# Layer 0 of a four-layer graph network: the order of all engines made from a list of steps, and the far entries' weighting moved to ScalarE

## The chip, the cores and the metric

The kernel runs on one core of a Trainium2 chip. The metric is the device time in microseconds of one execution. In the profile's names PE is TensorE (PEld its weight loads), DVE is VectorE, ACT is ScalarE, POOL is GpSimd and SP is SyncE; SP issues most DMAs, and POOL issues the indirect ones.

## The reference, cut to what matters

`x` is 2708 x 128, `adj` is 2708 x 2708 with some 2.3% of entries other than zero. Four layers follow each other, each closed by a residual and a normalization. Only layer 0 is touched:

```python
s = node_feats @ msg_w[:, :D].T
d = node_feats @ msg_w[:, D:].T
messages = jax.nn.gelu(s[:, None, :] + d[None, :, :] + msg_b, approximate=False)
aggregated = jnp.einsum('ijd,ij->id', messages, adj)
combined = jnp.concatenate([node_feats, aggregated], axis=-1)
new_feats = combined @ upd_w.T + upd_b
h = jax.nn.gelu(new_feats, approximate=False) + node_feats
```

A gelu is taken for each pair of rows (i, j) whose `adj[i, j]` isn't zero, of `s[i] + d[j] + b`, and the results are summed over j with the weights `adj[i, j]`.

## The kernel before, in words

**Tiling.** Layer 0 works on 22 row tiles of 125 rows (5 groups of 25), and within a tile on 22 column blocks of 124 columns: 484 blocks. For each row and block the first five entries other than zero get a slot; what is past the fifth is a "far" entry, of which a row has up to sixteen, found by their values.

**One block.** PE fills one of three two-bank tiles `sl` in PSUM: `begin` (L953) writes the row's `s` into all slots, `pick` (L960) adds `d` and the weight of the chosen columns through one-hot matrices `S` (ten matmuls). ACT takes the gelu out of `sl` into `g` (L1042). DVE's `weigh` (L1026) takes the weights out of the same `sl` into `W`. `add_up` (L977), once for two blocks, sums `g` with `W` into `acc`. A slot tile is free for the next `begin` when both have read it.

**One tile ahead.** For the next row tile the columns' third `at` and the rows `ar` are loaded by SP; DVE makes `mask` (L817), PE counts ranks (L825 for columns, L866 for rows), ACT casts them to `rk` (L826), DVE makes the five slot matrices `S` of each third (L845) and the parts of the weights `dA` (L838). `past` (L877, L879) keeps the entries past the fifth in `o` and counts them, `largest_of` and `largest` (MAX8) find the sixteen largest as `v`.

**Far entries.** `where` (L915, FIND_INDEX8) finds their places, eight at a time; `start_far` (L910) loads the row's `s` eight times into one of three buffers `far`, `fetch` (L919) adds eight gathered rows of `d` by indirect DMAs from POOL, `far_gelu` (L925, ACT) follows for all eight, and `far_sum` (L931, L933) multiplies each with its weight and adds it to `extra`, one DVE instruction for each of the sixteen. `turn` (L939 to L942, PE) brings `acc` and `extra` into `aggT`, `close` (L945) copies it out. `check` (L899 to L906) counts, in eight small DVE instructions a tile, rows with more far entries than sixteen or with equal values.

**Order.** The instructions of this part stand in the order in which the program issues them. Before, a loop over the 484 blocks issues `begin` (for two blocks), `pick`, the gelu, the block before's `weigh`, then every other step whose hand-written block number has come:

```python
for n in range(OV // 8):
    yield b - 1 + n * 9, lambda n=n: self.start_far(n)
    yield b + 2 + n * 9, lambda n=n: self.fetch(n)
    yield b + 15 + n * 13, lambda n=n: self.far_gelu(n)
    for k in range(8):
        yield b + 17 + n * 13 + k // 2, lambda n=n, k=k: self.far_sum(n * 8 + k)
yield b + 36, self.turn
```

After the last block the update of all rows follows (L1007 to L1016), with the last tile's second far gelu, far sums and turn between its first steps. Layers 1 to 3 follow.

Of the kernel before, what the change touches and what calls it, by code (L numbers as in the profile page):

```python
# [14 lines left out]
F32 = mybir.dt.float32  # L15
# [7 lines left out]
P = 128  # L23
# [47 lines left out]
class Step:  # L71


    def __init__(self, engine, cost, emit, after, rank, group, ahead, table, cells, bank, then):
        self.engine, self.cost, self.emit, self.after, self.rank = engine, cost, emit, after, rank
        self.group, self.ahead, self.table, self.cells, self.bank, self.then = group, ahead, table, cells, bank, then
        self.end = None

# [94 lines left out]
def gnn_stack(ctx: ExitStack, tc: tile.TileContext, t, out: bass.AP):  # L173
# [378 lines left out]
    with ExitStack() as l0:  # L552
# [10 lines left out]
        with ExitStack() as msg:  # L563
# [28 lines left out]
            nc.vector.memset(spread, 0.0)  # L592
# [4 lines left out]
            nc.vector.tensor_copy(spread[:, :, :RG], ident[:, :LR].rearrange("p (c i) -> p c i", c=NC))  # L597

            bad = mp.tile([P, LT], F32, name="bad")
# [3 lines left out]
            with tc.tile_pool(name="pre0", bufs=1) as pp:  # L603
                trif = pp.tile([JB, P], F32, name="trif")
                nc.vector.memset(trif, 1.0)
                nc.gpsimd.affine_select(
                    out=trif[:, :JB], in_=trif[:, :JB], compare_op=ALU.is_gt, fill=0.0, base=0,
                    pattern=[[1, JB]], channel_multiplier=-1)
                nc.vector.scalar_tensor_tensor(
                    trif[:, :JB], ident[:JB, :JB], EDGE, trif[:, :JB], op0=ALU.mult, op1=ALU.add)  # L610
                nc.vector.tensor_copy(tri, trif)


# [11 lines left out]
            lp = msg.enter_context(tc.tile_pool(name="load", bufs=3))  # L625
            ap_ = msg.enter_context(tc.tile_pool(name="rowsof", bufs=3))
            mk = msg.enter_context(tc.tile_pool(name="masks", bufs=2))
            sp = msg.enter_context(tc.tile_pool(name="ranks", bufs=3))
            op_ = msg.enter_context(tc.tile_pool(name="past", bufs=1))
            gp = msg.enter_context(tc.tile_pool(name="fetch", bufs=3))  # L630
            vp = msg.enter_context(tc.tile_pool(name="values", bufs=3))
            up = msg.enter_context(tc.tile_pool(name="sums", bufs=2))
            ep = msg.enter_context(tc.tile_pool(name="slots", bufs=6))
            p_misc = msg.enter_context(tc.tile_pool(name="ps_misc", bufs=1, space=PSUM))
            p_slot = msg.enter_context(tc.tile_pool(name="ps_slot", bufs=1, space=PSUM))
            p_out = msg.enter_context(tc.tile_pool(name="ps_out", bufs=1, space=PSUM))
            sl_all = [p_slot.tile([P, 2, BANK], F32, name=f"sl{n}") for n in range(3)]
            for v in sl_all:
                nc.vector.memset(v, 0.0)
# [7 lines left out]
            xT = aggT  # L647

            def turn_x():
                for n, (a, b) in enumerate(spans(0, NT, 4)):  # L650
                    ps = sl_all[n % 3][:, n // 3, :]
                    for i in range(a, b):
                        r = rows[i]
                        nc.tensor.transpose(ps[:, (i - a) * P:(i - a) * P + r], x[:r, i, :], ident[:r, :r])
                    w = min(b * P, N) - a * P
                    (nc.scalar.copy if n % 2 else nc.vector.tensor_copy)(xT[:, a * P:a * P + w], ps[:, :w])

            class Piece:


                def __init__(self, n):
                    self.n = n
                    self.b0, self.b1 = 4 * n, min(4 * n + 4, NB)
                    self.a0, self.a1 = 4 * n, min(4 * n + 4, NT)

                def products(self):
                    b0, b1, a0, a1 = self.b0, self.b1, self.a0, self.a1
                    psd, pss = (sl_all[(2 * self.n + k) % 3][:, 0, :].rearrange("p (b d) -> p b d", d=D)
                                for k in range(2))
                    d = self.d = ep.tile([P, NC, D], F32, name="g")[:JB, :b1 - b0, :]  # L670
                    room = gp.tile([P, 8, D], F32, name="far")
                    s = self.s = room[:, :a1 - a0, :]
                    parts = room[:, 4:, :].rearrange("p i d -> p (i d)").bitcast(FP16)
                    self.parts = parts.rearrange("p (q i d) -> p q i d", q=2, d=D)[:, :, :a1 - a0, :]
                    if N < b1 * JB:
                        nc.vector.memset(d, 0.0)
                    if N < a1 * P:
                        nc.vector.memset(s, 0.0)
                    for b in range(b0, b1):
                        r = min(JB, N - b * JB)  # L680
                        nc.tensor.matmul(psd[:r, b - b0, :], xT[:, b * JB:b * JB + r], msg_d, start=True, stop=True)
                    for i in range(a0, a1):
                        nc.tensor.matmul(pss[:rows[i], i - a0, :], xT[:, i * P:i * P + rows[i]], msg_s,
                                         start=True, stop=True)
                    full = min(b1, NFB) - b0
# [4 lines left out]
                    self.hi, self.lo = (v[:, b0:b1, :, :D] for v in dA)  # L690
                    nc.scalar.activation(self.hi[:, :, 0, :], d, AF.Copy, scale=D_SCALE)
                    self.spread(self.hi)
                    for a, b, r in groups():
                        if a0 <= a < a1:
                            nc.vector.tensor_tensor(s[:r, a - a0:b - a0, :], pss[:r, a - a0:b - a0, :],
                                                    over_tiles(msg_br, b - a, r), op=ALU.add)
                    nc.scalar.activation(self.parts[:, 0], s, AF.Copy, scale=D_SCALE)
                    nc.sync.dma_start(out=s_tab[a0 * P:a1 * P, :].rearrange("(n p) d -> p n d", p=P), in_=s)
# [4 lines left out]
                def spread(self, v):  # L703

                    nc.gpsimd.tensor_copy(v[:, :, 1:, :], v[:, :, 0:1, :].to_broadcast(
                        [JB, self.b1 - self.b0, NC - 1, D]))

                def update(self):
                    ps = p_out.tile([P, PB, D], F32, name="acc")
                    u = ep.tile([P, NC, D], F32, name="g")[:, :self.a1 - self.a0, :]  # L710
                    if N < self.a1 * P:
                        nc.vector.memset(u, 0.0)
                    for a, b, r in groups():
                        if self.a0 <= a < self.a1:
                            for i in range(a, b):
                                nc.tensor.matmul(ps[:r, i - self.a0, :], xT[:, i * P:i * P + r], upd_x,
                                                 start=True, stop=True)
                            nc.vector.tensor_tensor(u[:r, a - self.a0:b - self.a0, :],
                                                    ps[:r, a - self.a0:b - self.a0, :],
                                                    over_tiles(upd_b, b - a, r), op=ALU.add)  # L720
                    nc.sync.dma_start(out=u_tab[self.a0 * P:self.a1 * P, :].rearrange("(n p) d -> p n d", p=P), in_=u)

                def rests(self):
                    b0, b1, a0, a1 = self.b0, self.b1, self.a0, self.a1
                    lo = self.lo
                    nc.vector.scalar_tensor_tensor(self.parts[:, 1], self.s, D_SCALE, self.parts[:, 0], op0=ALU.mult,
                                                   op1=ALU.subtract)
                    nc.vector.scalar_tensor_tensor(lo[:, :, 0, :], self.d, D_SCALE, self.hi[:, :, 0, :], op0=ALU.mult,
                                                   op1=ALU.subtract)
                    self.spread(lo)  # L730
                    for q in range(2):
                        nc.sync.dma_start(out=sq_tab[q, a0 * P:a1 * P, :].rearrange("(n p) d -> p n d", p=P),
                                          in_=self.parts[:, q])

            def preparation():
                yield -NB - 9, turn_x
                for n, b in enumerate((-26, -22, -14, -10, -6, -2)):
                    piece = Piece(n)
                    yield b, piece.products
                    yield b + 2, piece.update  # L740
# [1219 lines left out]
```

## Time and profile before

| | us |
|---|---|
| median of 3 runs | 1880.32 (1880.05 to 1880.57) |
| the profiled execution | 1879.03, its span 1877.3 |
| layer 0, steady part | 100 to 780 us: 414 of 484 block gelus |
| layer 0, last sums on PE | up to 857.4 us |

The page gives busy shares for the span: PE 84%, DVE 76%, ACT 53%, POOL 35%. They mix four layers with different limits, so they say little on this change; the views by stretch say more. In the strip of 40 slices each digit is the busy share of a slice in tenths; one slice is 46.9 us, and layer 0 fills the first 18 or 19. In the groups of instructions the columns are line, engine, operation, what is written from what, the count, the busy time in us and the mean of one in ns, then the idle time before them and what ended it.

### The profile page before, as it was taken

The page shows a single profiled execution, that of the slowest core. Times are in us where ns is not written, and L with a number is a line of the kernel's source. Part 1 is how long each engine was busy: PE and PEld are TensorE (multiplying, and loading weights), DVE is VectorE, ACT ScalarE, POOL GpSimd, SP SyncE. Part 2 cuts the span into 40 slices and gives each one's busy share as a digit, 9 for nine tenths or more (in the row PEclk, how much of TensorE's full clock was granted, in tenths as well). Part 3 has the DMA queues.
Part 4 walks back from the last instruction along what each step waited for, and adds up shares of the span by engine and source line. Part 5 has one row for each costly group of instructions (what it writes and reads, how often), then busy time and mean ns, then how long its engine had stood idle before and what let it go on. Part 6 is the DMA issues. An engine that isn't in the chain of part 4 may idle for free.

```text
span 1877.3 us, 36661 instructions
## 1 busy us (share of the span) xinstructions
PE 1581.1 (84%) x14033; PEld 921.2 (49%) x14033; DVE 1432.4 (76%) x3609; ACT 999.4 (53%) x1538; POOL 653.2 (35%) x429
## 2 busy tenths in 40 slices
PE   4889999999999999884799995568888897299995
PEld 4666666666666666663444442312322343044542
DVE  7899999999999999976588885748886782860104
ACT  3556666666666666544344443568886862430003
POOL 5667767777777776664100000010000100000000
PEclk9899999999999999997899998658997798599998
DMA  8757666666666766543044410032333554354431
GB/s 223 167 117 153 127 144 145 135 145 128 147 135 137 151 129 139 101 104 104 0 154 161 164 64 1 9 118 89 139 139 117 171 174 169 118 207 148 148 123 32
DMA packets 234895, 238.29 MB, mean 127 GB/s; under 512 B 28844, under 2 KB 219630, under 8 KB 228122
## 3 DMA queue, kind: packets, MB, share of 16 engines
q1 hardware_dynamic: 183670, 212.18, 36.2%
q0 software_dynamic: 51040, 23.68, 10.6%
q8 instruction: 112, 1.84, 0.4%
q14 instruction: 73, 0.60, 0.1%
HBM read 220.65 MB, written 15.15 MB: 126 GB/s over the span
## 4 chain that ended last, share of the span: by engine, by line
PE 38%; DVE 7%; ACT 6%; issue 1%; DMA 0%; ACTq 0%; DVEq 0%
PE acc L1857 11%; PE lg L1245 5%; PE acc L1252 5%; PE accV L1585 5%; PE ps L1513 4%; PE accO L1589 2%; PE ps L1568 1%; ACT arena L1519 1%; DVE arena L1547 1%; PE ps L1514 1%; ACT x L379 1%; DVE arena L1571 1%; PE ps L447 1%; PE ps_w L1213 1%; ACT arena L1540 0%
## 5 line engine op out<-in xcount | busy, mean ns | idle before, releaser
L919 POOL DMA_INDIRECT far<-d_tab,ix x352 | 583.1, 1657 | 217.3 <-issue 97.0
L1042 ACT ACTIVATE g<-sl 128x640 f32<-128x640 f32 x484 | 335.4, 703 | 297.3 <-PE sl L960 272.5
L960 PE MATMUL sl<-dA,S 124*128 124x153 f16 x4840 | 380.9, 233 | 0.0
L960 PEld LDWEIGHTS <-S 124*128 124x128 f16 x4840 | 326.0, 98 | 72.0 <-issue 69.8
L977 PE MATMUL acc<-g,W 128*32 128x128 f32 x4840 | 194.5, 280 | 15.5 <-DVE W L1026 13.5
L953 PE MATMUL sl<-s,same 50*128 50x459 f16 x968 | 150.5, 333 | 17.8 <-DVE W L1026 15.5
L977 PEld LDWEIGHTS acc<-g,W 128*32 128x32 f32 x4840 | 117.4, 109 | 70.4 <-DVE W L1026 27.5
L1026 DVE TENSOR_TENSOR W<-sl,own 128x125 f32<-128x125 f32 x484 | 131.2, 275 | 21.6 <-ACT g L1042 21.6
L1500 POOL TENSOR_TENSOR arena<-arena,off 128x128 f32<-128x128 f32 (+1 forms) x22 | 23.0, 1049 | 350.3 <-DMA arena<-in_adjT 245.1
L845 DVE TENSOR_SCALAR S<-rk 124x1000 f16<-124x1000 bf16 (+1 forms) x330 | 141.4, 455 | 0.0
L1246 ACT ACTIVATE w<-lg,row_L_gnn_gate_bias 128x512 f32<-128x512 f32 (+1 forms) x132 | 83.4, 636 | 108.2 <-PE lg L1245 107.0
L915 DVE FIND_INDEX8 ix<-v,o 128x8 uint32<-128x2728 f32 x44 | 131.8, 2994 | 0.0
L1585 PE MATMUL accV<-arena,X 128*128 128x512 f32 (+4 forms) x264 | 123.3, 587 | 6.5 <-DVE arena L1551 6.5
L1245 PE MATMUL lg<-qT,mT 128*128 128x512 f32 (+2 forms) x264 | 121.2, 548 | 3.6 <-ACT w L1246 3.1
L1252 PE MATMUL acc<-w,both 128*128 128x512 f32 (+2 forms) x264 | 121.2, 547 | 0.0
L449 DVE TENSOR_TENSOR g<-ps,row_L_gnn_b 128x512 f32<-128x512 f32 (+2 forms) x14 | 7.9, 573 | 147.4 <-PE ps L447 147.3
L933 DVE SCALAR_TENSOR_TENSOR extra<-far,v,extra 128x128 f32<-128x128 f32 x330 | 114.6, 347 | 6.8 <-ACT far L925 0.5
L1513 PE MATMUL ps<-XT 128*128 128x512 f32 (+8 forms) x150 | 91.0, 696 | 32.2 <-ACT arena L1519 26.5
L1857 PE MATMUL acc<-at,x 128*128 128x512 f32 (+2 forms) x156 | 66.2, 575 | 48.5 <-ACT x L379 48.5
L1247 DVE TENSOR_TENSOR w<-w,at 128x512 f32<-128x512 f32 (+1 forms) x132 | 82.6, 626 | 27.1 <-ACT w L1246 27.0
L877 DVE SCALAR_TENSOR_TENSOR o<-ps,ar 128x496 f32<-128x496 f32 x132 | 82.0, 621 | 12.2 <-DMA ar<-in_adj 6.8
L884 DVE MAX8 cand<-o 128x8 f32<-128x248 f32 x242 | 90.4, 412 | 0.0
(359 smaller groups left out, 2494.2 us busy)
## 6 DMA issues: line engine op xcount, KB each, us to landing
at<-in_adjT SPq DMA_DIRECT2D x42, 1354.0 KB
ar<-in_adj SPq DMA_DIRECT2D x105, 248.0 KB
far<-s_tab SPq DMA_DIRECT2D x44, 512.0 KB
at<-in_adjT SPq DMA_DIRECT2D x42, 448.0 KB
arena<-in_adjT SPq DMA_DIRECT2D x21, 704.0 KB
arena<-in_adjT SPq DMA_DIRECT2D x21, 650.0 KB
held<-in_adjT SPq DMA_DIRECT2D x7, 1354.0 KB
f_tab<-arena SPq DMA_DIRECT2D x10, 704.0 KB
```

The source lines that it names most:

```text
L845: nc.vector.tensor_scalar(self.S[h][:, :n, :, k * RG:(k + 1) * RG], self.rk[h][:, :n, :LR].rearrange("p b (c i) -> p b c i", c=NC), EDGE + ...
L915: nc.vector.max_index(ix, self.v[:, n * 8:n * 8 + 8], self.o.rearrange("p b j -> p (b j)"))
L919: nc.gpsimd.indirect_dma_start(out=self.far[n][:, k, :], out_offset=None, in_=d_tab[:, :], in_offset=bass.IndirectOffsetOnAxis(ap=self.ix[ ...
L953: nc.tensor.matmul(columns_of(sl, 0, DA)[:, a:e, :], same[p], self.s3[p, :e - a, :], start=True, stop=False)
L960: nc.tensor.matmul(columns_of(sl, 0, DA)[:, c, :], self.S[h][:, n, c, :], dA[q][:, b, c, :], start=False, stop=q == 1 and c in (2, NC - 1))
L977: nc.tensor.matmul(self.acc[q:q + 32, k, :], W[:, c, :], g[:, c, :], start=b == 0 and k == 0, stop=ends)
L1042: nc.scalar.activation(g, columns_of(sl, 0, D), AF.Gelu, scale=1.0 / D_SCALE)
L1245: nc.tensor.matmul(lg, mT[:, j * P:j * P + r], qT[:, a:b], start=True, stop=True)
L1252: nc.tensor.matmul(acc[k], mrow[:rows[j], j, :], ws[j][:rows[j], a:b], start=j == 0, stop=j == NT - 1)
L1513: nc.tensor.matmul(ps, XT[:, self.js], XT[:, c], start=True, stop=False)
L1585: nc.tensor.matmul(Pair.acc[0][:, a:b], X[:self.r, self.j, :], self.w_[:, a:b], start=first, stop=last)
L1857: nc.tensor.matmul(acc[k], src[:rows[j], j, :], at[:rows[j], a:b], start=j == order[0], stop=j == order[-1])
```

## The change

The order of layer 0's main part is no longer written by hand. Every step is added to a list with its engine, a cost, a due number and the keys that it reads and writes; `Order.run` goes through time by these costs and, whenever an engine is free, issues its ready step with the lowest due number. The costs and due numbers serve for the order alone. Buffers come from fixed lists (as many of each as before) in place of pools. The gelu and the `weigh` of a slot tile both "write" the slot's key, so `weigh` comes after the gelu in the list. `begin` is a step for each slot tile. The far entries are scaled on ACT, one instruction for each of the sixteen (`far_weigh`), and then added on DVE by halving, for both halves of a tile at once. The checks of all tiles are made once, at the last tile, from kept `v` and counts; `past` copies the raw count. Clears of `ar` and of the last third's `at` are done once on POOL at the start; `tri` is made in the room of `spread`.

```diff
+class Order:
+    LATENCY, TURN = 0.12, 0.1
+    def add(self, engine, cost, emit, due, reads=(), writes=(), lag=0.0, take=None, give=None, kind=None):
...
+    def run(self, buffers):
...
+                while mine:
+                    due, s = heapq.heappop(mine)
+                    if s.take and not (freed[s.take] and min(freed[s.take]) <= now):
+                        held.append((due, s))
+                        continue
...
+                    s.emit()
...
+            DUE = {"load": -20.5, "load_s": 25, "load_row": -11, "start_far": 153.5, "rank": -19, "rank_row": -16,
+                   "begin": -0.3, "pick": 0, "add_up": 2.5, "turn": -26.5, "out": 10, "cast": 17.5, "a_hi": 58.5,
+                   "gelu": 36, "far_weigh": 68.5, "close": 126, "far_gelu": 57, "weigh": -67, "largest": -48,
+                   "index": -38, "mask": -11, "far_sum": -34.5, "past": -5, "max": -2.5, "a_lo": 1, "S": 1,
+                   "fetch": 125}
...
-                def far_sum(self, k):
-                    w, f = self.v[:, k:k + 1], self.far[k // 8][:, k % 8, :]
-                    if k == 0:
-                        self.extra = up.tile([P, D], F32, name="extra")
-                        nc.vector.tensor_scalar(self.extra, f, w, None, op0=ALU.mult)
-                    else:
-                        nc.vector.scalar_tensor_tensor(self.extra, f, w, self.extra, op0=ALU.mult, op1=ALU.add)
+                def far_weigh(self, n, k):
+                    f = far_all[(self.t * (OV // 8) + n) % 3][:, k, :]
+                    nc.scalar.activation(f, f, AF.Copy, scale=self.v[:, n * 8 + k:n * 8 + k + 1])
+                def far_sums(self, fars):
...
+                    yield "DVE", 1.12, plus(a, a, b), keys[1], keys[0]
+                    yield "DVE", 0.61, plus(a[:, :4, :], a[:, :4, :], a[:, 4:, :]), (), keys[0]
+                    yield "DVE", 0.33, plus(a[:, :2, :], a[:, :2, :], a[:, 2:4, :]), (), keys[0]
+                    yield "DVE", 0.2, plus(self.extra, a[:, 0, :], a[:, 1, :]), keys[0], [("extra", self.t % 2)]
...
+                            add("POOL", 1.56, fetch, due + DUE["fetch"] + k,
+                                reads=[("ix", f), ("far", f), *(("d_tab", j) for j in range(6))],
+                                writes=[("far", f, k)], lag=4.5)
...
+                        add("ACT", 0.6, functools.partial(nc.scalar.activation, g_all[g], columns_of(sl_all[sl], 0, D),
+                                                          AF.Gelu, scale=1.0 / D_SCALE), block + DUE["gelu"],
+                            writes=[("sl", sl), ("g", g)])
+                        add("DVE", 0.2, functools.partial(weigh, sl_all[sl], W_all[W]), block + DUE["weigh"],
+                            writes=[("sl", sl), ("W", W)])
...
+            add("SP", 0.1, U.load, (LT - 1) * NB + 7, reads=[("u_tab", n) for n in range(6)],
+                writes=[("o", m) for m in range(-(-NB // PB))], lag=6.0)
+            add_check((LT - 1) * NB + 8)
             with tc.manual_schedule():
+                order.run({"misc": 1})
...
+                def far_sums():
+                    for k in range(8):
+                        R[-1].far_weigh(OV // 8 - 1, k)
+                    for _, _, emit, _, _ in R[-1].far_sums(R[-1].fars):
+                        emit()
```

## The prediction

> **What bounds the kernel now.** The page's strip of slices comes first: layer 0 is its left half, up to about 860 us.
>
> ```profile
> PE   4889999999999999884799995568888897299995
> ...
> DVE  7899999999999999976588885748886782860104
> ```
>
> PE and DVE both read 9 there, so the strip alone doesn't decide. I then took busy time by stretch: the steady part, and a piece of the last row tile, which has no next tile to prepare (columns: length; PE, PEld, DVE, ACT, POOL busy with counts; PE clock; DMA share; GB/s).
>
> ```profile
> 100.00:780.00 680.00, 631.08 (x9751) 453.67 (x9749) 658.34 (x1892) 431.96 (x711) 505.00 (x303) 1.00 0.65 137
> ...
> 837.00:856.00 19.00, 19.00 (x322) 14.06 (x318) 10.04 (x36) 11.78 (x18) 15.96 (x11) 1.00 0.61 122
> ```
>
> The steady stretch holds 414 slot gelus, 22 to a tile: a tile takes 680/414 x 22 = 36.14 us. DVE is busy 96.8% of it, 35.0 us a tile. The waits of this stretch say the same (total us, times, longest):
>
> ```profile
> ACT g L1042 <- PE sl L960: 227.1, 214, 2.8
> ...
> PEld acc L977 <- DVE W L1026: 20.3, 37, 1.1
> PEld L866 <- DVE count L879: 18.0, 19, 1.0
> ...
> PE sl L953 <- DVE W L1026: 13.6, 38, 0.5
> ...
> PEld L825 <- DVE mask L817: 11.0, 19, 0.6
> ```
>
> ACT waits for PE, PE waits for DVE: the four DVE rows give 63 us over 18.8 tiles, 3.4 us a tile. DVE is the bound; PE is next. How near PE is shows in the last tile, where DVE has slack (timeline: start, length, what):
>
> ```profile
> 837.75 1.51 PE L960 MATMUL sl<-dA,S 124*128 124x153 f16 x20
> 839.19 0.86 PE L977 MATMUL acc<-g,W 128*32 128x128 f32 x24
> 839.99 0.56 PE L953 MATMUL sl<-s,same 50*128 50x459 f16 x4
> 840.48 1.51 PE L960 MATMUL sl<-dA,S 124*128 124x153 f16 x20
> ```
>
> From 837.75 to the start of the next-but-one pair at 843.00 PE runs two pairs of blocks without a wait: 2.63 us a pair, 28.9 us for eleven. A full tile adds 5.5 rank products at 0.31, 22 row products at 0.31 for four, and one turn of 0.68 (start to start in the timeline of 400 to 437), less about 0.5 where a rank product replaces the 0.09 gap ahead of the sums: **PE's floor is 32.5 us a tile**, 3.6 below what a tile takes.
>
> **What the Trainium skill says.** *Perfetto Trace Analysis*, "Identifying the Most-Contended Engine": occupancy names the bound for DVE and ACT, matmul busy time is a bad measure for PE. The trace agrees: PE shows 93% busy, but by starts works 32.5 of 36.14 us (90%). *VectorE: DVE Perf Modes*, "The TRN2 errata": an fp32 tensor_tensor add takes (N+151)/0.96 ns; for N=512 that is 691, the trace's L1014 has 684. *ScalarE: Activation LUTs*, "What ACT_TABLE_LOAD costs": an activation takes 186 ns + 0.833 N, plus 93 per per-partition operand, and neighbours overlap by 93. The trace agrees: L379, 128 columns with scale and bias, has 477 against 479. *GPSIMD Engine Reference*, "Key points": POOL shares its SBUF interfaces with DVE instructions that have two SBUF inputs; the fetch L919 has a median of 1552 ns and a maximum of 2427.
>
> **The change, part by part, per tile.** The groups of 60 to 780 us (20 tiles) give what is removed and what may bind next:
>
> ```profile
> L919 POOL DMA_INDIRECT far<-d_tab,ix x320 | 532.7, 1665 | 185.6 <-issue 89.0 <-DVE W L1026 75.1 <-ACT rk L826 9.0
> ...
> L1042 ACT ACTIVATE g<-sl 128x640 f32<-128x640 f32 x438 | 303.6, 703 | 259.7 <-PE sl L960 240.5 <-DVE cand L884 11.1 <-DVE S L845 7.0
> ...
> L933 DVE SCALAR_TENSOR_TENSOR extra<-far,v,extra 128x128 f32<-128x128 f32 x292 | 101.3, 347 | 5.5
> ```
>
> 1. Far sums. Sixteen DVE instructions go: (101.3 + 5.5 of L931)/20 = 5.3 us. Four adds of 1024, 512, 256 and 128 columns come: by the formula 1.22+0.69+0.42+0.29, less the 0.085 overlap seen in the timeline each: 2.3. DVE saves 3.0. ACT gains sixteen 128-column scalings with one per-partition operand: 186+107+93-93 = 0.29 us each, 4.7. ACT was 431.96/680 x 36.14 = 23.0; it becomes 27.7. That is hidden under PE's 32.5; uncovered it would be 4.7 a tile on the gelus, which are queued behind the scalings on ACT, and the next slots' `begin` waits for those.
> 2. The check. Eight DVE instructions a tile fill 1.1 us (429.44 to 430.54); they go, and nine stand once in the last tile (by the same formula, at 330 to 484 columns for the wide ones, some 3.5 us), where DVE is busy only half the time (10.04 of 19 us): nothing, or 3.5 once.
> 3. Clears of `at` and `ar` that shrink or go: 0.2. The plain copy for `count` costs what the two-operation one did (0.12).
> 4. DVE becomes 35.0 - 3.0 - 1.1 - 0.2 = 30.7 us a tile, below PE's 32.5. **PE becomes the bound.**
> 5. The order. PE's matmuls are the same. In the built program a `begin` may now stand alone, and the weight step follows its gelu on DVE at highest priority. No view of before shows what the new order leaves of PE's stalls. Bounds: 0, or all 3.6 us. I take 1.3: two FIND_INDEX8 of 3.0 us still stand in DVE's way (they cost PE 0.19 + 0.42 at 423.6 and 427.0), and far gelus now stand where ACT may wait for fetches: from the end of the index search 15 fetches at 1.67+0.30 and 4.2 us landing make 33.8, with 3.5 from the gelu ahead of the search 37.3 us; ACT's order leaves 24 blocks, 36.9 us at 33.8 a tile. About half a microsecond. **A tile takes 33.8** (32.6 to 35.3), 2.34 less; 21 tiles: **-49**.
> 6. The start. First pick is at 54.0 us. The built program puts all products first, then only the first third's slots and two rows before it; DVE has about 26.6 us of work from 15.7 on, so with before's 4 us of waits the pick comes near 46. But some 9 us of DVE work is deferred into tile 0, which has 3 us of DVE slack more than before. I take -4 (0 to -8; four more POOL clears and early loads could eat it). SP issues the first thirds and rows ahead of the table stores; they land in the same stretch, whose DMA share was 0.99.
> 7. The end. The last tile's index search stands three blocks later (after the fourth weight step, not the first): 16 fetches at 1.85 start 4.2 us later, and they end last:
>
> ```profile
> 863.16 1.06 ACT L925 ACTIVATE far<-far 128x1024 f32<-128x1024 f32 x1 [2.35 <-DMA far<-d_tab,ix]
> ...
> 864.25 3.06 DVE L933 SCALAR_TENSOR_TENSOR extra<-far,v,extra 128x128 f32<-128x128 f32 x8 [0.50 <-ACT far L925]
> ```
>
>    The 3.06 us become 8 x 0.29 on ACT and 2.3 on DVE, 4.7: +1.6. DVE's row steps for the update queue behind that sum. **+6** (+3 to +9). On SP the last `far` load is now behind the 22-tile `u_tab` load; the first half's eight fetches cover both.
>
> Layers 1 to 3 only start earlier: nothing.
>
> Sum against the profiled execution's own 1879.0 (span 1877.3 and 1.7 around it): -49 - 4 + 6 = -47, so 1832; the median shown is 1.3 above that execution: **1833**.
>
> **The rivals.**
> - *Far entries bind.* The sums of both halves come together, so a half's buffer is held until both are done; the load for the next tile's second half waits for that and stands behind another 512 KB load on SP. Loop: sums 2.5, issue 0.5, landing 5.6 (59.1 to the first fetch at 64.7), seven fetches and landing 18.0, gelu and scalings between gelus 6: 32.6, and 512 KB at 137/0.65 GB/s in front, 2.5: 35.1 a tile. For it: POOL alone needs 16 x 1.97 = 31.5. Against: the front load is issued 1.2 us sooner and fewer two-input DVE instructions disturb POOL. 21 x 1.04 less, and the 2 that start and end add: 1860.
> - *The same loop, longer: slower.* The planner counts a fetch as 1.56, not 1.97, and a pair on PE as 2.3, not 2.63. If SP, which issues in order, holds the `far` pair behind a row load whose buffer isn't free (such issues took up to 3.4 us in before), the loop is up to 38; ACT stands at the far gelu with 22 gelus behind it, and PE behind those. Past 36.1 a tile the change loses. Midway, at 37.2: 21 x 1.06 + 2, so 1904. Against: the row load ahead of the pair waits for a DVE step already done by then.
> - *It doesn't do what it says.* DVE's queue stays full because the weight step must now wait for gelus behind scalings; a tile stays at 36.1: 1882. ACT's 8 us of idle left speak against it.
>
> **How the numbers follow.** A measurement of this kernel can tell about 0.2%, 4 us. PE-bound 0.68, far-bound 0.16 (both faster), unchanged 0.04, slower loop 0.12. PE-bound at its best (32.6 a tile, -74 -6 +4) is 1804; at 35.3 a tile with the start's gain gone and +8 at the end, 1870. I give 1804 to 1868; the slower loop and half of the unchanged case are left out.
>
> **What would show it.** Right: in the steady part DVE falls to about 91% busy, ACT rises to 82%, PE's waits for DVE shrink from 3.4 to near 1 us a tile, scalings take about 0.385 us each, and the last turn, 10 us after PE's last sums in before (857.4 to 867.5), comes about 15 after them. Wrong: DVE above 95% (step 4), ACT's largest wait being on fetches (step 5, far-bound), SP issues of `far` taking microseconds (slower loop), a first pick later than 54 (step 6).

## The result, and the profile after

The changed kernel takes **1877.76 us** (median of 20 runs, 1864.08 to 1882.63), the kernel before 1880.55 (median of 20, 1878.84 to 1883.03): a ratio of 0.9976, interval 0.9961 to 0.9991. The forecast was 1833, in 1804 to 1868. The profiled execution of the changed kernel took 1882.63, the longest of its twenty (span 1880.8), so its trace stands at +3.5 us against that of before where the medians stand at -2.8.

The strip of 40 slices, PE and DVE:

```profile
PE   5889999999999999973699995568988897199995
...
DVE  8788888988888989966588885848886783760104
```

DVE has mostly left the 9s for 8s, PE has not risen. Busy time by stretch, with the steady part and a piece of the last row tile (columns: length; PE, PEld, DVE, ACT, POOL busy with counts; PE clock; DMA share; GB/s):

```profile
100.00:780.00 680.00, 638.32 (x9851) 466.80 (x9848) 593.47 (x1492) 526.39 (x1032) 530.33 (x310) 0.98 0.67 140
831.00:850.00 19.00, 17.32 (x275) 12.43 (x274) 9.29 (x26) 12.89 (x27) 15.73 (x11) 1.00 0.65 140
```

The steady stretch now holds 419 slot gelus, so DVE works 593.47 x 22/419 = 31.2 us a tile (35.0 before) and ACT 27.6 (23.0). The work went where it was forecast to go, and the tile did not follow. The waits of 100 to 780 us say why (us in total, times, longest):

```profile
ACT g L147 <- PE sl L1110: 81.4, 107, 2.1
...
DVE W L1127 <- ACT g L147: 68.9, 66, 6.5
...
ACT far L1023 <- DMA far<-d_tab,ix: 32.7, 19, 6.7
...
PE sl L1102 <- DVE W L1127: 26.3, 36, 2.0
...
ACT far L1023 <- issue: 15.8, 10, 3.1
PE misc L928 <- DVE count L934: 14.0, 14, 6.2
```

ACT stood at the far gelu for 0.7 us in before; now it stands there for 32.7 + 15.8 us (a wait marked "issue" ends at nothing that the profile shows; that these end at a fetch too is read from the place, and experiment 1, with half of the fetches, has neither). DVE's weight step waits for the gelu behind it (8.8 us before, 68.9 now), and PE's `begin` for that. One such stand in the timeline:

```profile
424.06 1.55 POOL L997 DMA_INDIRECT far<-d_tab,ix  x1 [0.30 <-ACT g L147]
...
430.12 1.06 ACT L1023 ACTIVATE far<-far 128x1024 f32<-128x1024 f32 x1 [3.10 <-issue]
...
432.23 0.29 DVE L1127 TENSOR_TENSOR W<-sl,own 128x125 f32<-128x125 f32 x1 [1.36 <-ACT g L147]
...
432.57 0.35 PE L1102 MATMUL sl<-s,same 50*128 50x459 f16 x2 [1.74 <-DVE W L1127]
```

The last of sixteen fetches starts at 424.06, the gelu on its half at 430.12; the next slot gelu is done at 432.2, the weight step behind it follows, and PE has lost 1.74 us.

**Tile by tile.** The start of the first FIND_INDEX8 of each tile (its search) marks the tiles; in the changed kernel it stands a few blocks later in a tile than in before, and later still in the first. From the third search to the twentieth a tile takes 36.02 us in before and **35.31** in the changed kernel. The table follows the two profiled executions along the program (us):

| up to | before | after | difference so far |
|---|---|---|---|
| first pick | 54.0 | 61.1 | +7.1 |
| first search | 58.9 | 73.9 | +15.0 |
| third search (two tiles) | 131.9 | 144.6 | +12.7 |
| twentieth search (17 tiles) | 744.2 | 744.9 | +0.7 |
| last search (two tiles) | 827.3 | 823.2 | -4.1 |
| last sums of blocks | 857.4 | 852.5 | -4.9 |
| last turn | 867.5 | 866.0 | -1.5 |
| layer 1's weight transposes | 887.0 | 884.0 | -3.0 |
| layer 1's first gate matmul | 931.8 | 934.9 | +3.1 |

The +15.0 at the first search isn't all delay, since that search has moved. By slot gelus, which are the same 484 in both, the first comes 7.1 us later than in before, the 23rd (a tile on) 5.5 and the 45th 8.8.

Three things eat the gain: the start, ACT at the far gelu, and the passage into layer 1. The start and the passage in the timeline of the changed kernel:

```profile
55.38 0.27 DVE L778 MEMSET g<- 128x256 f32 x1 [7.63 <-DMA u_tab<-g]
...
61.08 2.77 PE L1110 MATMUL sl<-dA,S 124*128 124x153 f16 x20
...
852.47 4.73 PE L1171 MATMUL sl<-w_L_upd_wT,aggT 128*128 128x128 f32 x40
865.97 0.90 PE L1052 MATMUL misc<-spread,extra 128*128 128x160 f32 x2 [8.76 <-DVE extra L1035]
...
884.01 0.45 PE L1335 MATMUL ps<-ident,w_L_gnn_W_q 128*128 128x128 f32 x1 [9.19 <-DVE bad_n L1236]
...
907.17 1.30 SPq L1382 DMA_DIRECT2D at<-in_adjT  x3
907.18 0.49 DVE L1337 COPY wT<-ps 128x128 f32<-128x128 f32 x2 [1.13 <-ACT x L460]
```

DVE stands 7.63 us in front of a clear whose buffer is still being stored. Layer 1's first copy comes after the last instruction of layer 0's norm; in before it stood at 887.50, and the first `at` load at 875.01.

**The clock.** The granted clock of PE was 0.98 in the steady part, 1.00 in before and 0.99 in experiment 5. Were all of PE's 32.9 us a tile (experiment 1) 2% longer for it, that would be some 0.7 us, an estimate from these figures; experiment 5, at 0.99, has 1.6 us a tile less, so the clock is not the main part.

### The profile page after: what moved, and what is told of

Its sections match the earlier page's. It is cut to its first block, busy times and chain, and to the rows that moved or that the text cites. A ratio compares the mean times of both kernels' runs of the same rounds, so it can differ in the third digit from the quotient of the medians.

```text
span 1880.8 us, 36540 instructions
## 1 busy us (share of the span) xinstructions
PE 1580.3 (84%) x14033; PEld 930.7 (49%) x14033; DVE 1360.8 (72%) x3129; ACT 1099.9 (58%) x1890; POOL 673.4 (36%) x433
## 3 DMA queue, kind: packets, MB, share of 16 engines
q1 hardware_dynamic: 183670, 212.18, 36.2%
## 4 chain that ended last, share of the span: by engine, by line
PE 37%; DVE 6%; ACT 6%; issue 1%; ACTq 0%; DVEq 0%
PE acc L2003 10%; PE lg L1391 5%; PE acc L1398 5%; PE accV L1731 5%; PE ps L1659 4%; PE accO L1735 2%; PE ps L1714 1%; ACT arena L1665 1%; PE ps L1660 1%; DVE arena L1693 1%; DVE arena L1717 1%; ACT arena L1686 1%; ACT x L460 1%; PE ps L528 1%; PE ps_w L1359 1%
## 5 line engine op out<-in xcount | busy, mean ns | idle before, releaser
L997 POOL DMA_INDIRECT far<-d_tab,ix x352 | 600.7, 1706 | 210.7 <-issue 99.7
L1110 PE MATMUL sl<-dA,S 124*128 124x153 f16 x4840 | 393.4, 233 | 0.0
L1110 PEld LDWEIGHTS <-S 124*128 124x128 f16 x4840 | 333.3, 99 | 68.6 <-issue 63.4
L1118 PE MATMUL acc<-g,W 128*32 128x128 f32 x4840 | 187.4, 280 | 0.2 <-DVE W L1127 0.2
L1102 PE MATMUL sl<-s,same 50*128 50x459 f16 x968 | 152.2, 335 | 34.9 <-DVE W L1127 33.5
L913 DVE TENSOR_SCALAR S<-rk 124x1000 f16<-124x1000 bf16 (+1 forms) x330 | 120.7, 415 | 9.1 <-ACT g L147 8.6
L1027 ACT ACTIVATE far<-far,v 128x128 f32<-128x128 f32 x352 | 119.5, 396 | 1.4
L1393 DVE TENSOR_TENSOR w<-w,at 128x512 f32<-128x512 f32 (+1 forms) x132 | 82.6, 626 | 27.1 <-ACT w L1392 27.0
L893 ACT CAST rk<-misc 124x512 bf16<-124x512 f32 x132 | 72.2, 547 | 33.9 <-PE misc L890 33.9
```

The costliest lines, as they stand in the source:

```text
L997: nc.gpsimd.indirect_dma_start(out=far[:, k, :], out_offset=None, in_=d_tab[:, :], in_offset=bass.IndirectOffsetOnAxis(ap=ix[:, k:k + 1], ...
L1102: nc.tensor.matmul(columns_of(sl, 0, DA)[:, a:e, :], same[p], self.s3[p, :e - a, :], start=True, stop=False)
L1110: nc.tensor.matmul(columns_of(sl, 0, DA)[:, c, :], S_all[h][:, n, c, :], dA[q][:, b, c, :], start=False, stop=q == 1 and c in (2, NC - 1))
L1118: nc.tensor.matmul(acc_all[q:q + 32, k, :], W_all[W][:, c, :], g_all[g][:, c, :], start=b == 0 and k == 0, stop=ends)
```

## The experiments

The theory: **the far chain**. From a tile's search to the far gelu of its second half there are sixteen fetches; in ACT's fixed order the gelu stands too few blocks behind the search, and everything on ACT, then DVE, then PE stands with it. Rivals: the list's order itself makes the engines wait for one another; the scalings load ACT too much; DVE was never the bound.

**1. Half of the fetches, same order.**

```diff
                             def fetch(k=k, far=far, ix=ix):
+                                if k % 2:
+                                    return
```

> The changed kernel with every second fetch of a far half left out (4 of 8 are issued, the other four far entries keep only their source row; the built order of every other instruction is unchanged). Far-chain theory: the last fetch of a half then lands some 8 to 16 us earlier, ACT no longer stands at the far gelu (2.6 us a tile in the changed kernel, plus what stands behind it), and a tile falls from 35.7 to 33.0-34.0 us, so the time to 1825-1845. Rival, the list's order itself makes PE, DVE and ACT wait for one another: the tile stays within 0.5 of 35.7 and the time at 1865-1880.

Measured: 1818.03 (1810.1 to 1819.3), ratio 0.9672 (0.9658 to 0.9686). The tile is **32.92** us, all from the third to the twentieth search between 32.9 and 33.2. ACT has no wait at the far gelu left. With the order of every other instruction unchanged, the list alone isn't what costs; the fetches in it are. (POOL and the DMA engines have less to do here as well; experiment 5 keeps all of the fetches.) It also sizes PE's floor: 32.9 where the prediction had 32.5, with PE 99% busy from 100 to 780 us.

**2. The start: a buffer of its own for the last update piece.**

```diff
-                u = g_all[gu][:, :a1 - a0, :]
+                k_u = "agg" if n == 5 else ("g", gu)
+                u = agg if n == 5 else g_all[gu][:, :a1 - a0, :]
```

> The changed kernel with the last update piece in a buffer of its own (the one of the summed row, free until the end of tile 0), so that its clear on DVE no longer waits for an earlier store. If that clear is what puts the first pick at 61.1 us: the first pick comes at 53-55 us and the time falls by 5-8 us. If DVE and POOL disturbing one another in 20-45 us is the cause, the pick stays past 59 and the time falls by under 2 us.

Measured: 1882.91 (1867.73 to 1892.98), ratio to before 1.0001 (0.9986 to 1.0015). The first pick came at 54.72, as expected; the time did not follow. The first search came at 76.8, later than the changed kernel's 73.9. The clear was the cause of the late pick, not of the late search: in this trace ACT then stands 7.74 us, up to 64.69, for a store of `u_tab`, which experiment 11 takes up.

**3. The passage into layer 1: two pools.**

```diff
             mp = msg.enter_context(tc.tile_pool(name="msg", bufs=1))
+            ep = msg.enter_context(tc.tile_pool(name="ends", bufs=1))
...
-            o_all = mp.tile([P, max(NB * JB, NT * D)], F32, name="o")
+            o_all = ep.tile([P, max(NB * JB, NT * D)], F32, name="o")
```

(likewise `g_all`, `tot` and the small tiles of the check)

> The changed kernel with the tiles that the final norm still uses (the gelu buffers, the o buffer, tot and the check's small tiles) in a second pool, the rest as it was. If layer 1 starts late because its first tiles take the place of one pool that is busy until the norm's end: its first adjacency load is issued before 890 us (907.2 in the changed kernel, 875.0 before), its transposes start 8-11 us earlier, and the time falls by 5-7 us. If the norm's own chain sets the start of layer 1: under 1 us.

Measured: 1875.45 (1869.96 to 1876.71), ratio 0.9965 (0.9952 to 0.9978). The load is issued at 868.31, layer 1's transposes of `x` start at 895.20 (908.33), and from its weight transposes to its first gate matmul there are 45.3 us where the changed kernel has 50.9: **5.6 us**. In the time only 2.3 of it shows against the changed kernel's scatter; the trace carries the reading: layer 1 waited for the whole pool.

**4. The far gelu later in the list.**

```diff
-                                writes=[("far", f, k)], lag=4.5)
+                                writes=[("far", f, k)], lag=5.5)
```

> The changed kernel with one number of the list changed: a fetch counts as landed 5.5 us after it, not 4.5, which puts the second half's far gelu three gelus later in ACT's order (the 31st after the tile's first instead of the 28th) and the far sums two blocks later. Far-chain theory: ACT's waits at the far gelu fall below 1 us a tile, and a tile falls to 33.8-34.8 us, the time to 1838-1860, unless the buffer that the sums free two blocks later makes the next tile's fetches late (then POOL shows waits and the gain is under 10 us). Rival (the order itself): within 5 us of 1878.

Measured: 1877.80 (1870.69 to 1890.16), ratio 0.9991 (0.9974 to 1.0009); a tile of 35.41. ACT's wait at the second half's gelu is gone (0.3 us over 18 tiles, 27.1 in the changed kernel). The first half's, whose place is as it was, stays (26.3 us, 16.7). The buffer that was named as the exception shows in the timeline of this kernel:

```profile
436.82 1.22 DVE L1035 TENSOR_TENSOR far<-far,far 128x1024 f32<-128x1024 f32 x1
...
438.07 1.90 SPq L989 DMA_DIRECT2D far<-s_tab  x2
...
445.15 2.65 POOL L997 DMA_INDIRECT far<-d_tab,ix  x1 [1.99 <-DVE W L1127]
```

The first halving add frees a buffer at 438.04, SP loads the next source rows into it, and POOL, which had done the first half's fetches, stands until 445.15. But the second half's gelu, which these fetches feed, no longer waits, so this delay reaches nothing behind POOL. What does reach PE is the first half's gelu:

```profile
409.67 1.06 ACT L1023 ACTIVATE far<-far 128x1024 f32<-128x1024 f32 x1 [2.35 <-DMA far<-d_tab,ix]
...
412.36 0.29 DVE L1127 TENSOR_TENSOR W<-sl,own 128x125 f32<-128x125 f32 x1 [2.36 <-ACT g L147]
```

From the third to the twentieth search PE has gaps of more than 0.25 us with a sum of 27.5 us; 20.0 of them end within 4 us of the start of a first half's gelu, none within 4 us of a second half's. By this trace the half that was left in its place holds the tile, not the buffer. Whether the buffer would bind if both gelus stood later, with three buffers, was not run.

**5. A fourth far buffer, and the far gelus of both halves later** (the 21st and 31st gelu, where they were the 18th and 28th). The room comes from the last third's `at`, `rk` and `S`, cut from 8 blocks to 6.

```diff
-several(3, [P, 8, D], F32, "far")
+several(4, [P, 8, D], F32, "far")
-add("POOL", 1.56, fetch, ... lag=4.5)
+add("POOL", 1.7, fetch, ... lag=9.5)
```

> The changed kernel with a fourth buffer for the far entries (its room comes from the last third's at, rk and S tiles, cut from 8 blocks to the 6 they hold) and the list's fetch at 1.70 us with 9.5 us to landing, which puts the second half's far gelu at the 31st gelu (28th in the changed kernel), the first half's at the 21st (18th) and the sums at block 34. Theory of two loops (ACT's place of the far gelu, and the buffer that the sums free): both are gone, and a tile falls to 33.0-34.3 us, the time to 1825-1850. If POOL's own rate or DMA time per fetch were the bound: a tile of 35 or more, above 1860.

Measured: 1858.18 (1856.69 to 1860.23), ratio 0.9877 (0.986 to 0.9893); a tile of **33.72**, most of them 33.5. The tile is in its range; the time is above it, with a first pick that fell back to 67.7 (the clear of experiment 2 now stands 11.15 us) and a passage into layer 1 as long as in the changed kernel. In the steady part:

```profile
100.00:780.00 680.00, 665.52 (x10280) 482.99 (x10279) 620.04 (x1552) 539.11 (x1078) 541.20 (x323) 0.99 0.72 144
```

PE is at 98%, DVE at 91%: the picture that the prediction drew, near its price (33.8).

**6. The fourth buffer alone.**

> The changed kernel with the fourth far buffer alone; the list's numbers are untouched, and the order built from them puts the far gelus at the 17th and 26th gelu of a tile (18th and 28th in the changed kernel). If ACT's place of the far gelu is what costs: waits at the far gelu grow, the tile is 35.7-37.5 us, the time 1875-1915. If the freed buffer is what costs: a tile of 33.5-34.5, 1835-1855.

Measured: 1913.31 (1907.63 to 1915.19), ratio 1.0166 (1.0145 to 1.0186); a tile of 36.82. More room lets the list put the far gelus at the 17th and 26th gelu, nearer to the search, and ACT stands longer (63.5 us of the steady 680 in waits that a fetch ended). So this run doesn't show the buffer by itself, and experiment 4 moved one half only: place and buffer together are enough, that both are needed is not shown.

**7. The change's work in the hand-written order.** Scaling on ACT and four adds behind the last of them; no check of each tile.

```diff
                     w, f = self.v[:, k:k + 1], self.far[k // 8][:, k % 8, :]
+                    nc.scalar.activation(f, f, AF.Copy, scale=w)
+                    if k == OV - 1:
...
+                            nc.vector.tensor_tensor(o, p, q, op=ALU.add)
```

> The kernel before with its order by hand, and only the work of the change in it: far entries scaled on ACT, four halving adds on DVE after the last scaling, and no check of each row tile (the check of counts and of equal values is left out). Its far gelus stand at about the 16th and 29th gelu after a search at the 1st, 27 gelus for the 16 fetches where the changed kernel has 24. If DVE was the bound as predicted and the far gelus' place spoils the changed kernel: DVE falls to about 31 us a tile, the tile to 33.5-34.8, the time to 1835-1860. If a lighter DVE is of no use in any order: 1872-1882.

Measured: 1919.14 (1918.12 to 1921.1), ratio 1.0202 (1.0185 to 1.0219); a tile of 37.71. My theory fell here: less work on DVE, room for the fetches (no wait at the far gelu), and slower than before. The timeline shows one piece of it:

```profile
419.39 2.41 DVE L936 TENSOR_TENSOR far<-far 128x1024 f32<-128x1024 f32 x3 [1.42 <-ACT far L929]
421.83 0.29 DVE L936 TENSOR_TENSOR extra<-far 128x128 f32<-128x128 f32 x1
...
422.64 0.62 PE L980 MATMUL acc<-g,W 128*32 128x128 f32 x13 [2.02 <-DVE W L1029]
```

DVE stands 1.42 us for the last scaling, adds for 2.7 us in one piece, and PE waits 2.02 us behind it.

**8. The list's order with the far sums left on DVE.**

```diff
-                        add("ACT", 0.29, lambda k=k: self.far_weigh(n, k), due + DUE["far_weigh"] + k / 2, reads=[("far", f)],
-                            writes=[("far", f, k)])
+                        add("DVE", 0.35, lambda k=k: self.far_weigh(n, k), due + DUE["far_weigh"] + k / 2, reads=each,
+                            writes=[("extra", self.t % 2)])
```

> The changed kernel (order from the list, one check) with the far entries weighted and summed on DVE, sixteen instructions as before the change. If the list's order alone is what costs, its far gelus stand as early as in the changed kernel and DVE has 3 us a tile more to do: a tile of 36-38 us, 1885-1930. If scaling on ACT were what holds ACT and PE up: a tile of 34.5 or less, under 1860.

Measured: 1982.22 (1977.74 to 1984.11), ratio 1.0531 (1.0513 to 1.0548), tiles between 33 and 55 us by their slot gelus up to the twentieth. Both expectations missed. The list's due numbers were not fitted to this work, so the run gives no sign that the scaling holds ACT up, and doesn't price the order by itself either.

**9 and 10. What DVE's and ACT's time is worth in the kernel before.** In 9 every second far sum is left out (DVE -2.65 us a tile), in 10 each far entry is multiplied by 1 on ACT (ACT +4.7).

```diff
-                        for k in range(8):
+                        for k in range(0, 8, 2):
```

> The kernel before with every second one of the sixteen far sums on DVE left out (eight entries of a row tile are not summed), nothing else changed: DVE has 8 x 0.35 = 2.65 us a tile less, ACT and the order stay. If DVE is the bound of the kernel before, as predicted: a tile falls by 2-2.6 us to 33.5-34.2, the time to 1825-1842. If the hand order's waits are what sets the tile: under 1 us a tile, 1860 or more.

> The kernel before with sixteen more ACT instructions a tile: each far entry is multiplied by 1 in place, two entries ahead of its sum, so that ACT has the 4.7 us of the change's scalings more and DVE's work is unchanged. If 4.7 us on ACT hide in its 13 us of idle time, as predicted: within 8 us of before. If each scaling holds up the gelu behind it and with it PE, whose next begin waits for that bank: 2-4 us a tile, so 1920-1965.

Measured: 9 takes 1848.82 (1847.08 to 1849.39), ratio 0.9838 (0.9812 to 0.9864), a tile of 34.42; 10 takes 1890.04 (1885.61 to 1896.35), ratio 1.0065 (1.0044 to 1.0086), a tile of 36.75. Both lie between their theories. Of 2.65 us taken from DVE the tile got 1.60 back, six tenths; of 4.7 us put on ACT it paid 0.73, a sixth. DVE was the bound, with a discount whose cause these runs don't show.

**11. All edits together, and then SP's order.** First the buffer, the place, the start and the pools at once:

> The changed kernel with four edits together: fourth far buffer, far gelu placed later (a fetch at 1.70 us, 9.5 us to landing), the last update piece in a buffer of its own, and the tiles of the final norm in a second pool. The first two alone gave 1858 with a first pick at 67.7 and layer 1's first load at 885 (its transposes follow the norm). If start and end now carry through because the fetch loop no longer sets the pace: the pick at 54-57 and layer 1 five us earlier, 1838-1847. If the loop takes the start back, as it did with the buffer alone: 1852-1858.

Measured: 1859.46 (1857.58 to 1861.5), ratio 0.9893 (0.9872 to 0.9913). The first pick came at 57.58, ten earlier than in 5, and tile 0 lost it:

```profile
62.41 0.36 SPq L991 DMA_DIRECT2D far<-s_tab  x1
62.87 0.56 SPq L812 DMA_DIRECT2D u_tab<-g  x1
...
67.67 2.10 ACT L147 ACTIVATE g<-sl 128x640 f32<-128x640 f32 x3 [7.86 <-DMA u_tab<-g]
```

The fourth slot gelu writes a `g` whose update piece is not stored yet; SP holds that store behind a load of far source rows whose buffer is still in use. So the load was put behind the stores in the list:

```diff
-                            reads=[("s_tab", k) for k in self.pieces],
+                            reads=[("s_tab", k) for k in self.pieces] + [("u_tab", k) for k in range(6) if t < 2] + [("v", 0, 0)] * (t == 1),
```

> The kernel with four edits (c1_all) and one more in the list: the first two row tiles' loads of far source rows are put behind the stores of the update table on SP. In c1_all the first pick came at 57.6 us, ten earlier than with the buffers alone, but ACT then stood 7.9 us at the fourth gelu for a store of the update table that SP held behind such a load, and tile 0 took 41.8 us. If SP's order is what takes the start's gain back: tile 0 at 33-36 us, the time at 1849-1855 (1859.5 in c1_all). If another wait takes its place in the first two tiles: 1856-1862.

Measured: **1837.61** (1836.74 to 1839.25), ratio 0.9769 (0.9756 to 0.9782), the fastest kernel here and better than I expected. First pick 54.99, first search 67.1 (78.8 in `c1_all`), a tile of 33.64 (34.24). By the 23rd slot gelu 11.7 us are won on `c1_all`, by the last 23.0: the start is about half of it, the shorter tiles are the other. In the steady part:

```profile
100.00:780.00 680.00, 662.69 (x10222) 481.49 (x10221) 615.35 (x1551) 533.15 (x1063) 539.73 (x321) 0.99 0.70 143
```

Why `c1_all`'s steady tile was 0.6 longer than this one's, with far gelus and sums at the same places, I did not trace.

**12. Both start edits in the changed kernel alone.**

> The changed kernel with both start edits and nothing else: the last update piece in a buffer of its own and the first far loads behind the update table's stores on SP. Three far buffers and the early far gelus stay. The first pick comes at 53-57 us (61.1 in the changed kernel). If the start's gain is its own: 1868-1874. If the fetches' loop sets the pace from the first tile on and takes it back, as with the buffer alone (1882.9): 1876-1884.

Measured: 1875.88 (1873.54 to 1879.06), ratio 0.9971 (0.9959 to 0.9983). First pick 54.3, first search 67.3, 6.6 earlier than in the changed kernel; at the last search 2.7 of it are left. The tile was 35.71 in this trace (35.31 in the changed kernel's), with the same waits at the far gelu. In these runs a head start paid where the fetches don't set the pace.

**13 and 14. What makes the hand order slow?** First the adds taken apart, one a block (with turn, source load and second fetches later so that nothing stands in front of a buffer in use); then in addition DVE's low half of `dA` one block later, since DVE stood up to 1.0 us for ACT at each.

```diff
+                    for k in range(4):
+                        yield b + 34 + k, lambda k=k: self.far_add(k)
```

> The hand order with the change's work (e7_hand_order, 1919; the check of counts and equal values is left out here too), its four halving adds taken apart: one a block from the block after the last scaling on, instead of all four behind that scaling; turn and close two blocks later, and the second half's source load and fetches five and three blocks later, so that SP does not stand in front of a buffer still in use. In e7_hand_order DVE stood 1.4 us for the last scaling, then added for 2.7 us in one piece, and PE waited 2.0 us a tile behind it. If that piece is what makes the hand order slower than before: PE's wait of 2 us a tile goes and the time is 1860-1890. If ACT's load or the held buffers are: 1905 or more.

> The hand order with the change's work and split sums (e11_split_sums, 1901.6; the check of counts and equal values is left out here too), with one step moved: DVE's low half of a third's adjacency one block later than ACT's high half asks, because DVE stood 1.0 us at each such step for ACT (31.8 us in the steady 680 us), a wait that the kernel before did not have. If these stands in a fixed order are what eats DVE's saving: the wait goes, a tile falls from 36.5 to 34.8-35.8 and the time to 1868-1890. If the stand only moves to the next step: 1895-1904.

Measured: 13 takes 1901.63 (1899.52 to 1901.98), ratio 1.0107 (1.0091 to 1.0122), a tile of 36.49, with a median of 36.24 (one of 39.9 at the start lifts the mean; before has 36.04): the time is 17.5 of the 38.5 us shorter than in 7. 14 takes 1902.47 (1899.36 to 1907.67), ratio 1.0124 (1.0102 to 1.0145), a tile of 36.60 (median 36.10). Its waits on DVE in the steady part:

```profile
DVE W L1033 <- ACT g L1049: 89.3, 60, 3.3
```

The 31.8 us at `dA` are gone, and the stand before the weight step has grown from 36.2 to 89.3. ACT's stands at the far gelu have grown too, from 11.5 to 30.9 us. The wait moved, the tile stayed.

Where the losses lie: the first slot gelu of the last tile comes 37.2 us later than in before in experiment 7, 6.2 in 13. So over the tiles the single piece, with what was moved along with it, was nearly all of the loss. The rest of 13's lies in the last tile and the end: its last turn comes 22.6 us later than in before, after a last fetch that starts at 878.4 (858.9 in before); the second fetches that this edit puts later make that likely, it was not tried apart. Why a tile of the hand order gains nothing from a lighter DVE stays open; that DVE stands in a fixed order for ACT is seen, what would cure it isn't.

## Why the prediction was wrong

- **Steps 1 to 4, the work: right.** DVE 31.2 us a tile (30.7 foreseen), ACT 27.6 (27.7); a scaling has a mean of 396 ns (385), by its group:

```profile
L1027 ACT ACTIVATE far<-far,v 128x128 f32<-128x128 f32 x352 | 119.5, 396 | 1.4
```

  Its pitch in the timeline is 0.29 to 0.30 us, as worked out. PE's floor was 32.5 in the prediction, 32.9 in experiment 1.
- **"DVE is the bound", read from 97% busy: right, but a busy share is no exchange rate.** *Perfetto Trace Analysis*, "Identifying the Most-Contended Engine", names the engine rightly (experiment 9 gains); its time counts by six tenths there. That the other engines' fixed orders wait for one another may be the reason; it is not shown.
- **Step 5, the far chain: the step that failed.** The mechanism was named, and priced at "about half a microsecond"; it cost 2.6 us of ACT a tile. The chain of the second half, term by term, foreseen and measured (means from the third to the twentieth search): from the gelu ahead to the end of the search 3.5, 3.7; search to first fetch nothing, 0.8; fifteen pitches 29.6, 30.5 (2.03 each); from the last fetch's start to the gelu 4.2, but 4.4 to 6.7 where ACT stands, 5.2 in the mean. That is 40.2 where it had 37.3, against 36.9 us of blocks: 3.3 short where it had 0.4. The first half's gelu wasn't priced at all; it stands too (0.9 us a tile, the second half's 1.5), and in experiment 4 most of PE's gaps lie behind it. *Perfetto Trace Analysis*, "DMA Instruction — SWDGE (GPSIMD)", says that the record of such a DMA on POOL ends with its descriptors, not with its data; the trace agrees (record over at 425.61, gelu at 430.12), so the landing had to be taken from waits, and from a spread of them.
- **The chance of 0.68 for "PE-bound".** With the wait gone (experiment 5) the tile is 33.72. The 33.8 had half a microsecond of that wait in it; without it the sum gives 33.3, and PE's floor was 0.4 higher, so that the two figures meet is in part luck. The margin at the far gelu was already -0.4 us at a landing of 4.2 us, the median that before's trace shows (3.2 to 6.7 over the run), and in the last tile of before ACT stood 2.35 us at a fetch; it should have been taken as the likeliest way to lose, and priced with a spread of landings. Of the prediction's own signs of error, the late first pick came true, and fetches are ACT's second wait, not its largest.
- **Step 6, the start: wrong sign.** -4 foreseen; the first pick came +7.1, the 45th slot gelu +8.8. The order of the steps was read, but not what the clear of a reused buffer waits for, nor that SP would hold that store behind a far load (experiments 2 and 11).
- **Step 7, the end: right in kind.** The last turn comes 13.5 us after the last sums (about 15 foreseen, 10.1 before).
- **"Layers 1 to 3 only start earlier: nothing": wrong.** 5.6 us, by the memory that layer 1's tiles take over (experiment 3). Buffers "from fixed lists in place of pools" was read as a change of nothing.
- **The rivals.** *Far entries bind*: POOL's stand for the freed buffer is seen in experiment 4, and its 35.4 us a tile is near the 35.1 foreseen; but PE's gaps there lie behind the first half's gelu, so the number doesn't show that loop. *The same loop, longer* holds a part of what happened: the planner's 1.56 us and 4.5 us for a fetch put the gelus too early, and ACT, then PE stood behind them. It came out at 35.3 a tile instead of 37.2, under its own breakeven of 36.1, so the kernel isn't slower. SP's part in it was not needed: its issues of `far` took 1.96 us a pair.

Why the time of the changed kernel scatters by 18.6 us over twenty runs, where the kernel of experiment 5 has 3.5 over four and `c2_far_after_u` 2.5 over five, was not tested. Stands at fetches aren't the whole of it: experiment 1, which has none, takes 1810.1 at a mean granted clock of 0.921 and 1817.2 to 1819.3 at 0.912 to 0.913. The four fastest of the twenty, 1864.1 to 1867.3, have 0.916 to 0.919, the others 0.907 to 0.916. So the scatter goes with the clock; which of the two drives the other is open, and effects of a few us (experiments 3 and 12) rest on their traces, not on the medians.

## What to carry to other kernels

An instruction that waits for a DMA, put into the fixed order of an engine that everything else hangs on, must stand behind the whole chain at its slow price, with slack for its spread, and every such instruction needs that price: here three blocks for both far gelus, with one buffer more, decided between 1878 and 1858 us. A tile that doesn't get shorter after a wait is gone has another one: look which wait the gaps of the bound engine lie behind (experiment 4). An order built from costs can move other steps when a buffer is added (experiment 6). What a queue issues first at the start, and what memory the next stage takes over at the end, are parts of a reordering and need a price of their own.

## What the runs showed of the hardware that I had not expected

- From the start of the last indirect fetch of a half on POOL to the gelu that waits for it there are 3.4 to 6.7 us in the changed kernel (second halves 4.4 to 6.7), of which the record on POOL mostly covers 1.55; the mean pitch of fetches in a row is 1.91 to 2.05 us in the seventeen traces, with eight of a half issued or four (2.02).
- DVE's two-input steps of 128x512 in the start took 1.99 to 2.75 us in four of five cases, and 0.68 in the fifth (in the kernel of experiment 5). Beside the four POOL copied `dA`: the longest ran from 39.50, the copy from 39.78 for 1.92 us. The fifth had 0.15 us alone, from 31.19 to a copy's start at 31.34. The two went together; it was not tried apart.
